# Products with C over two neighbouring PSUM banks, six of twelve on GpSimd, and an earlier turn of the last image, in a selective-scan and convolution hybrid

## The chip, the cores and the metric

The kernel runs on one core of a Trainium2 chip. The metric is the device time of one execution in microseconds (us); the kernel before was timed three times, and the median counts. The core's engines are named PE (TensorE), ACT (ScalarE), DVE (VectorE) and POOL (GpSimd); SP is the queue that issues every DMA here.

## The reference

Four images of 96 channels and 64 x 64 pixels go through four layers, and nothing is shared between images.

- Layer 0: group norm, a 1x1 projection to 192 channels and a depthwise 3x3 convolution with SiLU give u. u is read in four orders k: by rows (0), by columns (1), and both backwards (2 and 3). For each order and each of 192 channels a recurrence with 16 states runs over the 4096 positions. Then the four results, turned back to row order, are added, normalised and projected to 96 channels.

```python
delta = softplus(dts + dt_b)
dA    = exp(delta * A)                       # A is (order, channel, state)
h     = h * dA + (delta * u) * B[state]      # along the 4096 positions
y     = sum over states of h * C[state]  + Ds * u
```

- Layer 1: 1x1 expansion to 576 channels, depthwise 3x3 convolution, 1x1 projection, with a residual.
- Layer 2: layer norm, a 192-wide spectral block (Fourier transform over the positions, a diagonal complex product with ReLU, the inverse), then a feed-forward block 96-384-96 whose operands are rounded to 8-bit floats and whose sums are rounded to 16-bit floats.
- Layer 3: softmax-free attention, which is computed as a product with the sum of k v over all positions, and a second such feed-forward block.

## The kernel before

**The scan is cut into units and slots.** An order is scanned in 8 chunks of 512 positions, one chunk of one order of one image is a step, and a step has 12 units (`u` 0 to 11): there are 4 x 4 x 8 x 12 = 1536. A unit covers 128 rows (32 channel pairs times 4 states) and two channels `e` of a pair, so 2 x 512 elements in a row. `scans` (line 1120) writes the units out by hand, one a slot, in an order that no scheduler changes (line 1389). For slot `s` it issues in this order:

1. stores that were put off (`flush`, line 1266), then the loads of the next step's operands (`LOADS`, line 1164): each is a DMA of 512 KB that spreads `delta`, `du` or a pair of B and C rows over the 128 rows. The second B and C tile of a step is loaded at `u` 10, just ahead of its use.
2. `decays` of unit `s+1` on ACT (line 1180): for each `e` the last column of unit `s-1` is kept as the next chunk's start (`keep`, line 1203), then an exponential is written into a PSUM bank of its own out of four (`da`).
3. `product` of unit `s-1` on POOL (line 1215) if its `u` is in `POOL_C` = 1, 3, 6, 8, 10, and `inputs` of unit `s+2`, also on POOL (line 1176): `db` = delta u B, 128 x 1024.
4. `states` of unit `s` on DVE (line 1190): a scan for each `e`. For the other seven units of a step the scan is followed by the product with C, 128 x 512, for each `e` (line 1201).
5. `sums` on PE (line 1226) for a pair of units whose products were issued before; after the last pair of a pass ACT copies the result out (`yt`, line 1245), and its store is put off to the next slot's `flush`.

**Work beside the scan.** Everything else is written as generators grouped in stages (`plan`, line 1111): front of an image (its inputs to the scan), turn, conv, spectral, layer 2, layer 3. At the end of each slot `advance` (line 1353) takes steps from the stage at the head as long as their stated costs fit a budget for each engine (`SHARE`, line 55) and a total for the slot (`RATE`). Stages follow each other strictly; the stages of image b+1's front and of image b's later layers run beside scans of other images.

**The end.** Images are scanned in the orders 0, 1, 3, 2 (line 41). The turn (line 610) adds orders 0, 1 and 3 and the skip term of an image in row order, by matmuls with an identity, once three of its orders are scanned. `scan_outputs` (line 651) adds order 2 chunk by chunk, and the convolution takes two chunks at a time. For the last image the turn stands beside layer 3 of the third image, and its convolution is the last stage beside the scans; what is left of it, its spectral block, layer 2 and layer 3 run after the scan has ended, without a scan beside them (`alone`, line 1391). There all eight PSUM banks are handed out in turn, and in the feed-forward (line 856) ACT makes three passes for each of three 128-row parts: a copy to 16 bits (868), bias and ReLU (871), rounding to 8 bits (873).

Of the kernel before, what the change touches and what calls it, by code (L numbers as in the profile page):

```python
# [39 lines left out]

KORDER = (0, 1, 3, 2)

SCAN = {"rep_d": 3, "rep_g": 3, "rep_BC": 5, "db": 3, "hc": 5}
POOL_C = (1, 3, 6, 8, 10)
TMP, IN = 10, 5
# [8 lines left out]
RATE = 6.0  # L54
SHARE = {"pe": (3.0, 3.2), "act": (2.4, 3.0), "dve": (1.2, 1.7)}
NQ, NG, NPAIR = 4, HID // 32, H // 2
# [37 lines left out]
def hybrid_kernel(ctx: ExitStack, tc: tile.TileContext, a: dict):  # L94
# [15 lines left out]

    BANKS = {"mm": 3, "da": 4, "y": 1}

# [6 lines left out]
    def bank(tag="mm", turn=True):  # L119

        if alone and tag == "mm" and turn:
            tag = turns(alone)
        if tag == "mm":
            held_banks[0] += 1
        return psum.tile([128, CH], F32, name=f"ps_{tag}", tag=tag, bufs=BANKS[tag])

# [299 lines left out]

    def later(out, t):

        to_store.append((out, t))

    def flush():
        while to_store:
            store(*to_store.pop(0))

# [7 lines left out]

    def in_turn(items, make, matmuls, take, evict, depth=2):

        made = []

        def oldest():
            p, item, at = made.pop(0)
            yield take[:3] + (at,)
            evict(p, item)  # L450
            free()

        for n, item in enumerate(items):
            yield make[:3] + (n > 0,)
            p = bank()
            matmuls(p, item)
            made.append((p, item, clock[0]))
            if len(made) == depth:
                yield from oldest()
        while made:  # L460
            yield from oldest()
# [148 lines left out]
    def turn(b):  # L610

        im = b % 2
        while scanned[b] < 3 * NCH:
            yield wait(1)
        parts = [big("ya"), big("yb")]
        for lo in (0, 128):
            for t, k in zip(parts, (1, 3)):
                load(t[:, :L].rearrange("p (c l) -> p c l", c=NCH),
                     d_y[k][im][:, lo : lo + 128, :].rearrange("c p l -> p c l"))

            def fetch(c):
                y, u = (t[:, L + c % 4 * CH : L + c % 4 * CH + CH] for t in parts)
                load(y, d_y[0][im][c, lo : lo + 128])
                load(u[: min(128, DI - lo)], d_skip[b][c, lo : min(lo + 128, DI)])
                return y, u
# [5 lines left out]
            def added(p, of):  # L631
                c, (y, u) = of
                p = p[:m]
                for n, t in enumerate(parts):
                    rhs = t[:, :L].rearrange("p (w h) -> p h w", h=H)[:, c * RPC : (c + 1) * RPC, :]
                    mm(split(p), lhsT=add, rhs=rhs, start=n == 0, stop=False)
                mm(p, lhsT=add, rhs=y, start=False, stop=False)
                mm(p, lhsT=skip, rhs=u[: skip.shape[0]], start=False, stop=True)
# [5 lines left out]

            chunks = ahead(1, fetch, reversed(range(NCH)))
            first = next(chunks)
            yield wait(10)
            yield from in_turn(chain([first], chunks), pe(3.8, 1), added, ac(0.6), stored)
            yield wait(2)

    def scan_outputs(b, done):
# [3 lines left out]
        def fetch(c):  # L655
            out = []
            for of in (d_yt[b % 2][c], d_y[2][b % 2][c]):
                for part in (of[:128], of[128:]):
                    s = arrival("ypart")
                    load(s[: part.shape[0]], part)  # L660
                    out.append(s[: part.shape[0]])
            return out[0], out[2], out[1], out[3]

        coming = None
        for c in reversed(range(NCH)):
# [7 lines left out]
            for name, of in (("ident", parts[:2]), ("two", parts[2:])):  # L673
                yield pe(1.8, 1, name == "two")
                p = bank()
                for n, s in enumerate(of):
                    mm(p, lhsT=const(name, slice(0, s.shape[0])), rhs=s, start=n == 0, stop=n == 1)  # L677
                yield ac(0.6)
# [177 lines left out]
    def feed_forward(x, weights):  # L856
# [5 lines left out]
        for m in range(3):  # L862
# [6 lines left out]
            free()  # L869
            yield ac(0.65)  # L870
            act(acc, acc, AF.Relu, bias=bq[:, m : m + 1])  # L871
            yield ac(0.65)
            nc.scalar.activation(hq[:, m, :], acc, AF.Copy, saturate=False)  # L873
        yield pe(1.4, 1)
# [245 lines left out]
    def scans(stages):  # L1120
# [8 lines left out]
        for b in range(B):  # L1129
            for k in KORDER:  # L1130
                for n in range(NCH):
                    steps.append({"b": b, "k": k, "c": NCH - 1 - n if k >= 2 else n, "n": n, "BC": {}, "d": {}, "g": {}})
# [47 lines left out]
        def decays(x, last):  # L1180
            x["da"] = []
            for e in (0, 1):

                if last is not None:
                    keep(last, e)
                av = (x["step"]["k"] * NI + 2 * x["i"] + e) * NJ + x["j"]
                x["da"].append(bank("da"))
                act(x["da"][e], x["step"]["d"][x["i"]][:, e], AF.Exp, scale=aneg[:, av : av + 1])  # L1188

        def states(x):  # L1190
            step, u = x["step"], x["u"]
            order = slice(None, None, -1) if step["k"] >= 2 else slice(None)
            x["hc"] = pair("hc")
            x["h"] = [x["hc"][:, e] for e in (0, 1)] if x["pool"] else x["da"]
            for e in (0, 1):
                start = 0.0 if step["n"] == 0 else steps[x["number"] - 1]["last"][:, 2 * u + e : 2 * u + e + 1]
                nc.vector.tensor_tensor_scan(  # L1197
                    x["h"][e][:, order], x["da"][e][:, order], x["db"][:, e, order], start, ALU.mult, ALU.add
                )
                if not x["pool"]:  # L1200
                    x["made"] = nc.vector.tensor_mul(x["hc"][:, e], x["h"][e], x["step"]["BC"][x["j"]][:, 1])  # L1201

        def keep(x, e):
            step, u = x["step"], x["u"]
            if step["n"] < NCH - 1:
                if "last" not in step:
                    step["last"] = sp.tile([128, NI * NJ], F32, name="state")
                end = 0 if step["k"] >= 2 else CH - 1
                to = step["last"][:, 2 * u : 2 * u + 2]
                if not x["pool"]:  # L1210
                    nc.scalar.copy(to[:, e : e + 1], x["h"][e][:, end : end + 1])  # L1211
                elif e == 0:
                    nc.gpsimd.tensor_copy(to, x["hc"][:, :, end])  # L1213

# [11 lines left out]
        def sums(group):  # L1226
# [6 lines left out]
            for m in (1, 0):  # L1233
                x = group[m]
                for e in (1, 0):
# [3 lines left out]
                    if made is None:  # L1239
                        made = group[0]["made"]  # L1240
                        tc.add_manual_dep(done.ins, made.ins.name, mybir.DependencyInfo(
                            mybir.DependencyClass.Sync, mybir.DependencyReason.DATA), reason="sums")
            if last:
                yt = sp.tile([128, CH], F32, name="yt")
                nc.scalar.copy(yt, y)  # L1245
                to = d_y[step["k"]][step["b"] % 2][step["c"]]
                for m in (0, 1):
                    at = 128 * group[0]["pass"] + 64 * m
                    later(to[at : at + 64].rearrange("(p e) l -> e p l", e=2), yt[64 * m : 64 * m + 64])
                if group[0]["pass"] == 1:  # L1250
                    scanned[step["b"]] += 1

# [10 lines left out]
        for slot in range(len(units) + 6):  # L1263
            clock[0] = slot
            x = units[slot] if slot < len(units) else None
            flush()
            if x is not None:
# [10 lines left out]
                if x["number"] + 1 < len(steps) and x["u"] in LOADS:  # L1278
                    if x["u"] == 4:
                        need(steps[x["number"] + 1])  # L1280
                    fetch(steps[x["number"] + 1], LOADS[x["u"]])
            if slot + 1 < len(units):
                decays(units[slot + 1], units[slot - 1] if slot > 0 else None)
# [259 lines left out]
```

## Time and profile before

| what | value |
|---|---|
| time, median of 3 runs (lowest to highest) | 6703.26 us (6702.1 to 6710.55) |
| the profiled execution: its own time, its span | 6708.94 us, 6707.1 us |
| busy: PE, ACT | 4836.7 us (72%), 4357.4 us (65%) |
| busy: DVE, POOL | 5521.4 us (82%), 5173.5 us (77%) |
| DMA | 1121.42 MB, 167 GB/s over the span |
| first and last start of a DVE scan | 78.8 us, about 6126 us |

A time in the profile counts from the start of the span. A group of instructions is one line of the kernel on one engine with one kind of tiles: its busy time, the mean length of one, and the idle time of the engine just before them with what ended most of it. In a table by stretches each row is a stretch of the span with each engine's busy time in it and, in brackets, its instructions; then the clock granted to TensorE (1 is full), the share of the DMA engines' time in use and GB/s. POOL runs one `db` instruction (line 1178) for each unit, so the number of those in a stretch is its number of units.

### The profile page before, as it was taken

What the parts mean: (1) busy time and instruction counts of PE and PEld (TensorE: products, weight loads), DVE (VectorE), ACT (ScalarE), POOL (GpSimd) and SP (SyncE); (2) the same over time, 40 slices, a digit from 0 to 9 for tenths busy, and PEclk for the clock granted to TensorE, in tenths of its full rate; (3) what the DMA queues carried; (4) which work ended last, traced back from release to release, by engine and by line L of the source; (5) the groups of instructions that cost most, each with busy time, mean ns of one, the idle gap of its engine ahead of it and who ended that gap; (6) DMA issues with size and microseconds to landing.
All of it is one profiled execution on the core that took longest, in us unless ns stands there. A gap on an engine that the chain in (4) does not pass through costs nothing. (4 is left out here: it accounts for less than half of the span.)

```text
span 6707.1 us, 84452 instructions
## 1 busy us (share of the span) xinstructions
PE 4836.7 (72%) x27884; PEld 1777.4 (26%) x27884; DVE 5521.4 (82%) x5803; ACT 4357.4 (65%) x8296; POOL 5173.5 (77%) x2743
## 2 busy tenths in 40 slices
PE   7633857657987676775688777777887776779986
PEld 2100212111223531121122254221223532213562
DVE  5979899898999889889999988887999889895110
ACT  5743767765665577876556656866665677755367
POOL 4756878789999789977999988888999889894000
PEclk9755968768998787797799988878998887889997
DMA  5644555576644544455765454465644544563120
GB/s 185 193 157 142 180 188 188 180 239 231 188 152 143 181 154 145 156 187 187 257 208 165 147 168 167 144 208 176 193 151 151 193 157 145 202 230 101 38 82 27
DMA packets 438825, 1121.42 MB, mean 167 GB/s; under 512 B 73002, under 2 KB 74768, under 8 KB 437140
## 3 DMA queue, kind: packets, MB, share of 16 engines
q1 hardware_dynamic: 438388, 1116.02, 50.9%
q8 instruction: 222, 3.64, 0.2%
q14 instruction: 215, 1.76, 0.1%
HBM read 881.28 MB, written 239.01 MB: 167 GB/s over the span
## 5 line engine op out<-in xcount | busy, mean ns | idle before, releaser
L1178 POOL TENSOR_TENSOR db<-rep_g,rep_BC 128x1024 f32<-128x1024 f32 x1536 | 3600.2, 2364 | 551.0 <-DMA rep_BC<-bc 281.9
L1188 ACT ACTIVATE ps_da<-rep_d,aneg 128x512 f32<-128x512 f32 x3072 | 2067.3, 690 | 542.0 <-DVE hc L1197 404.5
L1197 DVE TENSOR_TENSOR_SCAN ps_da<-ps_da,state,db 128x512 f32<-128x512 f32 x1568 | 2007.1, 1280 | 237.3 <-ACT state L1211 154.5
L1216 POOL TENSOR_TENSOR hc<-hc,rep_BC 128x1024 f32<-128x1024 f32 x640 | 1510.8, 2361 | 91.0 <-DVE hc L1197 41.4
L1237 PE MATMUL ps_y<-hc,cst 128*32 128x512 f32 x6144 | 1026.7, 746 | 619.3 <-POOL hc L1216 348.2
L1197 DVE TENSOR_TENSOR_SCAN hc<-ps_da,state,db 128x512 f32<-128x512 f32 x1120 | 1371.1, 1266 | 70.3 <-ACT ps_da L1188 23.1
L1201 DVE TENSOR_TENSOR hc<-ps_da,rep_BC 128x512 f32<-128x512 f32 x1792 | 1239.2, 692 | 112.5 <-PE ps_y L1237 3.9
L1211 ACT COPY state<-ps_da 128x1 f32<-128x1 f32 x1568 | 247.2, 158 | 471.1 <-DVE hc L1201 466.3
L1237 PEld LDWEIGHTS ps_y<-hc,cst 128*32 128x32 f32 x6144 | 145.8, 119 | 1264.8 <-POOL hc L1216 556.6
L786 PE MATMUL ps_mm<-h,wd 128*32 128x512 f32 x3048 | 348.5, 593 | 7.0 <-ACT r L153 7.0
L1213 POOL COPY state<-hc 128x2 f32<-128x2 f32 x560 | 106.0, 189 | 306.9 <-DVE hc L1197 294.2
L531 PE MATMUL ps_mm<-xp,taps 128*128 128x512 f32 x576 | 293.6, 652 | 41.5 <-ACT xp L511 14.4
L1197 DVE TENSOR_TENSOR_SCAN ps_da<-ps_da,db 128x512 f32<-128x512 f32 x224 | 273.6, 1221 | 41.7 <-ACT state L1211 23.8
L582 PE MATMUL ps_mm<-xd,dtw 128*128 128x512 f32 x256 | 177.1, 783 | 162.2 <-ACT z L604 116.2
L763 PE MATMUL ps_mm<-wd,w 128*32 128x512 f32 x2032 | 261.2, 621 | 36.8 <-DMA wd<-x 11.9
L1245 ACT COPY yt<-ps_y 128x512 f32<-128x512 f32 x256 | 149.1, 582 | 151.1 <-PE ps_y L1237 145.1
L591 ACT ACTIVATE z<-ps_mm 128x512 f32<-128x512 f32 x192 | 114.3, 595 | 167.8 <-PE ps_mm L582 106.6
L912 PE MATMUL ps_mm<-wa,xp 128*64 128x96 f32 x1728 | 143.2, 327 | 103.1 <-DVE d L916 79.1
L597 DVE SCALAR_TENSOR_TENSOR ps_mm<-ps_mm,z 128x512 f32<-128x512 f32 x192 | 132.3, 689 | 99.1 <-ACT z L595 69.6
L1197 DVE TENSOR_TENSOR_SCAN hc<-ps_da,db 128x512 f32<-128x512 f32 x160 | 186.2, 1204 | 9.4 <-ACT ps_da L1188 9.0
L845 PE MATMUL ps_mm<-r,cst 128*128 128x512 f32 x206 | 138.8, 761 | 70.8 <-ACT acc L868 26.6
L569 PE MATMUL ps_mm<-ua,sel 128*128 128x512 f32 x128 | 101.3, 880 | 114.7 <-ACT z L604 91.1
(420 smaller groups left out, 6954.1 us busy)
## 6 DMA issues: line engine op xcount, KB each, us to landing
rep_BC<-bc SPq DMA_DIRECT2D x512, 512.0 KB
rep_g<-du SPq DMA_DIRECT2D x384, 512.0 KB
rep_d<-delta SPq DMA_DIRECT2D x384, 512.0 KB
y<-yt SPq DMA_DIRECT2D x512, 128.0 KB
du<-g SPq DMA_DIRECT2D x128, 256.0 KB
delta<-z SPq DMA_DIRECT2D x128, 256.0 KB
tab<-in_etab SPq DMA_DIRECT2D x128, 256.0 KB
du<-g SPq DMA_DIRECT2D x128, 128.0 KB
```

The source lines that it names most:

```text
L531: mm(p, lhsT=taps[:, t, 0:128], rhs=window(t, c + e), start=t == 0, stop=t == 8)
L582: mm(p, lhsT=dtw[:, o + 2 * part, 0:128], rhs=xd, start=True, stop=True)
L763: mm(p[32 * n : 32 * n + 32], lhsT=w1[:, 32 * g : 32 * g + 32], rhs=xin[:, n : n + 15 : 2, 1 : W + 1], start=True, stop=True)
L786: mm(p[32 * n : 32 * n + 32], lhsT=held["wd"][:, groups[i], o, dx, :], rhs=here[i][:, :, dx : dx + W], start=dx == 0, stop=dx == 2)
L1178: nc.gpsimd.tensor_mul(x["db"], x["step"]["g"][x["i"]], both(x["step"]["BC"][x["j"]][:, 0]))
L1188: act(x["da"][e], x["step"]["d"][x["i"]][:, e], AF.Exp, scale=aneg[:, av : av + 1])
L1197: nc.vector.tensor_tensor_scan(x["h"][e][:, order], x["da"][e][:, order], x["db"][:, e, order], start, ALU.mult, ALU.add)
L1201: x["made"] = nc.vector.tensor_mul(x["hc"][:, e], x["h"][e], x["step"]["BC"][x["j"]][:, 1])
L1211: nc.scalar.copy(to[:, e : e + 1], x["h"][e][:, end : end + 1])
L1216: x["made"] = nc.gpsimd.tensor_mul(x["hc"], x["hc"], both(x["step"]["BC"][x["j"]][:, 1]))
L1237: done = mm(y[32 * q : 32 * q + 32], lhsT=const("stack"), rhs=x["hc"][:, e], start=first or (x["pass"] == 0 and x["j"] == 0), stop=last or ...
L1245: nc.scalar.copy(yt, y)
```

## The change

- **Pairs of banks.** `da` becomes two buffers of two neighbouring banks each, one for a unit. Both exponentials of unit `s+1` now stand behind the whole of unit `s-1`; the last columns of both `e` are kept by one copy, and the product with C of a unit on DVE is one instruction of 128 x 1024 behind both scans. When no scan is beside, a `da` buffer gives one bank of its two, so that six banks are in turn.
- **Six products on POOL:** `u` 1, 3, 5, 7, 9, 11.
- **Loads ahead of stores:** `flush` moves behind the loads within a slot.
- **Budgets:** ACT's ceiling in a slot falls from 3.0 to 2.8, DVE's share rises from 1.2 to 1.5 and its ceiling from 1.7 to 2.0.
- **Last image:** its orders are scanned 1, 3, 0, 2. Its turn starts when orders 1 and 3 are done, and takes order 0 chunk by chunk as it comes; for channels 128 to 191 order 0 is added later, in `scan_outputs`, with one more load and matmul a chunk. A chunk counts as scanned when its store has been issued.
- **Feed-forward at the end:** with no scan beside, bias and ReLU go to DVE for all three parts, and the rounding to 8 bits for one of them.

```diff
-KORDER = (0, 1, 3, 2)
+KORDER = [(0, 1, 3, 2)] * (B - 1) + [(1, 3, 0, 2)]
-POOL_C = (1, 3, 6, 8, 10)
+POOL_C = (1, 3, 5, 7, 9, 11)
-SHARE = {"pe": (3.0, 3.2), "act": (2.4, 3.0), "dve": (1.2, 1.7)}
+SHARE = {"pe": (3.0, 3.2), "act": (2.4, 2.8), "dve": (1.5, 2.0)}
-    BANKS = {"mm": 3, "da": 4, "y": 1}
+    BANKS = {"mm": 3, "da": 2, "y": 1}
...
+        if tag == "da":
+            t = psum.tile([128, 2, CH], F32, name="ps_da", tag=tag, bufs=BANKS[tag])
+            return t[:, 0] if alone else t
...
     def turn(b):
-        while scanned[b] < 3 * NCH:
+        early = b == B - 1
+        while scanned[b] < (2 if early else 3) * NCH:
             yield wait(1)
...
-        for lo in (0, 128):
+        for lo in (128, 0) if early else (0, 128):
...
+            rows = not (early and lo == 128)
...
-                load(y, d_y[0][im][c, lo : lo + 128])
+                if rows:
+                    load(y, d_y[0][im][c, lo : lo + 128])
...
+            ready = (lambda n: scanned[b] >= 2 * NCH + min(n + 2, NCH)) if early and rows else (lambda n: True)
...
     def scan_outputs(b, done):
-            for of in (d_yt[b % 2][c], d_y[2][b % 2][c]):
-                for part in (of[:128], of[128:]):
...
+            yt, y0, y2 = (of[b % 2][c] for of in (d_yt, d_y[0], d_y[2]))
+            for part in (yt[:128], y2[:128], yt[128:], y2[128:]) + ((y0[128:],) if b == B - 1 else ()):
...
     def feed_forward(x, weights):
...
+            if alone:
+                yield dv(0.75)
+                nc.vector.tensor_scalar(acc, acc, bq[:, m : m + 1], 0.0, ALU.add, ALU.max)
+            else:
+                yield ac(0.65)
+                act(acc, acc, AF.Relu, bias=bq[:, m : m + 1])
+            if alone and m == 1:
+                yield dv(0.75)
+                nc.vector.tensor_copy(hq[:, m, :], acc, saturate=False)
+            else:
+                yield ac(0.65)
+                nc.scalar.activation(hq[:, m, :], acc, AF.Copy, saturate=False)
...
         def decays(x, last):
-            x["da"] = []
-            for e in (0, 1):
-                if last is not None:
-                    keep(last, e)
-                av = (x["step"]["k"] * NI + 2 * x["i"] + e) * NJ + x["j"]
-                x["da"].append(bank("da"))
-                act(x["da"][e], x["step"]["d"][x["i"]][:, e], AF.Exp, scale=aneg[:, av : av + 1])
+            if last is not None:
+                keep(last)
+            x["da"] = bank("da")
+            for e in (0, 1):
+                av = (x["step"]["k"] * NI + 2 * x["i"] + e) * NJ + x["j"]
+                act(x["da"][:, e], x["step"]["d"][x["i"]][:, e], AF.Exp, scale=aneg[:, av : av + 1])
...
         def states(x):
-                if not x["pool"]:
-                    x["made"] = nc.vector.tensor_mul(x["hc"][:, e], x["h"][e], x["step"]["BC"][x["j"]][:, 1])
+            if not x["pool"]:
+                x["made"] = nc.vector.tensor_mul(x["hc"], x["h"], both(x["step"]["BC"][x["j"]][:, 1]))
...
+                copy = nc.gpsimd.tensor_copy if x["pool"] else nc.scalar.copy
+                copy(step["last"][:, 2 * u : 2 * u + 2], x["h"][:, :, end])
...
             x = units[slot] if slot < len(units) else None
-            flush()
             if x is not None:
...
                     fetch(steps[x["number"] + 1], LOADS[x["u"]])
+            flush()
             if slot + 1 < len(units):
```

## The prediction

> **What bounds the kernel now.** I read the page's totals, then its groups, then a table by stretches, then two queues in order of time.
>
> ```profile
> PE 4836.7 (72%) x27884; PEld 1777.4 (26%) x27884; DVE 5521.4 (82%) x5803; ACT 4357.4 (65%) x8296; POOL 5173.5 (77%) x2743
> ```
>
> DVE leads and POOL is close behind, but the average spans stages of different kinds. What a unit costs on each engine is in the groups:
>
> ```profile
> L1178 POOL TENSOR_TENSOR db<-rep_g,rep_BC 128x1024 f32<-128x1024 f32 x1536 | 3600.2, 2364 | 551.0 <-DMA rep_BC<-bc 281.9
> ...
> L1197 DVE TENSOR_TENSOR_SCAN ps_da<-ps_da,state,db 128x512 f32<-128x512 f32 x1568 | 2007.1, 1280 | 237.3 <-ACT state L1211 154.5
> L1216 POOL TENSOR_TENSOR hc<-hc,rep_BC 128x1024 f32<-128x1024 f32 x640 | 1510.8, 2361 | 91.0 <-DVE hc L1197 41.4
> ...
> L1201 DVE TENSOR_TENSOR hc<-ps_da,rep_BC 128x512 f32<-128x512 f32 x1792 | 1239.2, 692 | 112.5 <-PE ps_y L1237 3.9
> L1211 ACT COPY state<-ps_da 128x1 f32<-128x1 f32 x1568 | 247.2, 158 | 471.1 <-DVE hc L1201 466.3
> ```
>
> POOL per unit: its busy time without 7 us of clearing, 5166/1536 = 3.36 us. DVE per unit is read from start to start, in order of time (start, length):
>
> ```profile
> 3641.93 1.29 DVE L1197 TENSOR_TENSOR_SCAN ps_da<-ps_da,state,db 128x512 f32<-128x512 f32 x1 [0.17 <-POOL db L1178]
> 3643.31 0.69 DVE L1201 TENSOR_TENSOR hc<-ps_da,rep_BC 128x512 f32<-128x512 f32 x1
> 3643.92 1.28 DVE L1197 TENSOR_TENSOR_SCAN ps_da<-ps_da,state,db 128x512 f32<-128x512 f32 x1
> 3645.23 0.69 DVE L1201 TENSOR_TENSOR hc<-ps_da,rep_BC 128x512 f32<-128x512 f32 x1
> 3645.84 2.45 DVE L1197 TENSOR_TENSOR_SCAN hc<-ps_da,state,db 128x512 f32<-128x512 f32 x2
> ```
>
> A unit with its product takes 3645.84 - 3641.93 = 3.91 us. One without takes 2.37 (the next such, from 3657.04, has its successor at 3659.41). So (7 x 3.91 + 5 x 2.37)/12 = 3.27 us, before work beside it. The table by stretches (length, busy PE, PEld, DVE, ACT, POOL, clock, DMA share, GB/s) shows which engine is full where:
>
> ```profile
> 663.00:1452.00 789.00, 533.32 (x1657) 147.44 (x1655) 712.13 (x761) 572.95 (x1074) 607.22 (x320) 0.81 0.58 187
> 1452.00:2090.00 638.00, 512.14 (x2595) 136.00 (x2598) 598.35 (x615) 384.68 (x768) 602.89 (x321) 0.89 0.59 195
> 2090.00:2291.00 201.00, 139.76 (x1734) 102.49 (x1730) 179.53 (x187) 110.97 (x212) 163.66 (x89) 0.79 0.48 159
> 2291.00:2834.00 543.00, 372.84 (x2147) 147.17 (x2140) 479.73 (x494) 421.03 (x805) 481.34 (x254) 0.78 0.48 156
> 4135.00:4585.00 450.00, 314.77 (x1036) 95.09 (x1033) 362.86 (x376) 311.06 (x611) 364.49 (x194) 0.80 0.52 172
> 6126.00:6319.00 193.00, 184.74 (x1248) 68.93 (x1240) 12.51 (x24) 70.06 (x109) 0.00 (x0) 0.98 0.11 32
> ```
>
> The rows are a front, turn and conv, spectral, layers 2 and 3, layer 3 with a turn, and the conv that is left when the scan has ended. In front DVE is at 90% and POOL at 77%; in turn and conv both are at 94%; elsewhere neither is over 90%; at the end PE is at 96%. With all such stretches and their units (the count of L1178 in each):
>
> | stage | us | units | us a unit |
> |---|---|---|---|
> | front | 1485 | 336 | 4.42 |
> | weights | 264 | 48 | 5.50 |
> | turn and conv, last scan | 2130 | 600 | 3.55 |
> | spectral | 679 | 168 | 4.04 |
> | layers 2 and 3 | 1039 | 276 | 3.76 |
> | layer 3 with turn | 450 | 108 | 4.17 |
>
> After 6126 us come conv 193, spectral 152, layer 2 139, layer 3 97 us.
>
> One more wait matters. First SP, then POOL, in order of time:
>
> ```profile
> 3616.67 3.07 SPq L1153 DMA_DIRECT2D rep_d<-delta  x2
> 3629.70 1.11 SPq L433 DMA_DIRECT2D y<-yt  x2
> 3630.92 0.56 SPq L1147 DMA_DIRECT2D rep_BC<-bc  x1
> ```
> ```profile
> 3635.68 2.38 POOL L1178 TENSOR_TENSOR db<-rep_g,rep_BC 128x1024 f32<-128x1024 f32 x1
> 3639.50 4.73 POOL L1178 TENSOR_TENSOR db<-rep_g,rep_BC 128x1024 f32<-128x1024 f32 x2 [1.44 <-DVE hc L1201]
> ```
>
> From 3619.7 SP stood in front of the `y` store until ACT had copied `yt` (3629.09 to 3629.68); the B/C load stood behind it, and POOL idled for the `db` that reads it. Counted by position in a step, 316 us of POOL's 551 us before `db` stand before that one, unit 2's.
>
> **What the Trainium skill says.** "VectorE: DVE Perf Modes", section on the TRN2 errata: an fp32 tensor_tensor takes (N+151)/0.96 ns. For 512 that is 691, the trace has 692; for 1024 it gives 1224 ns, my price of the merged product. "GPSIMD Engine Reference", 3.1: about 2.6 cycles an element for two inputs, so an estimate of 2.2 us for 1024 before dispatch; the trace has 2361 ns, which I use. "SBUF — State Buffer", Who interferes with whom: a DVE instruction with one SBUF input outside the two-port modes does not contend with GpSimd. The merged product reads C alone from SBUF, as now; the trace agrees in that `db` has minimum 2333 and median 2360 ns beside a busy DVE. I charge no contention.
>
> **The change part by part.**
>
> *POOL:* one product more in 12 units, 2361/12 = 197 ns, and 7/8 of a 189 ns state copy, 14 ns: 3.36 + 0.21 = 3.57 us a unit. With about 1% of waits, nothing goes below 3.60.
>
> *DVE:* a unit with a product now has its second scan 1.2 us behind the first, as in a unit without (2.45 us for two), the product 1.37 behind that (1.29 and the gap of 0.09 that the lines above show), and the next unit some 1.15 later (1.224 less the overlap of 0.08 that they show): 3.72 instead of 3.91. Six of each: (6 x 3.72 + 6 x 2.37)/12 = 3.05, so 0.22 us less. ACT's copies fall from 1568 to 672, 896 x 158 ns = 142 us or 0.09 a unit; its work is not what is full, so nothing.
>
> *By stage.* Turn and conv go onto POOL's floor: 3.55 to 3.60, +30 us. In layers 2 and 3 DVE waits for ACT and ACT for PE; of 0.22 the floor leaves 0.16, and I take 0.10, since these waits are uneven: -28. Layer 3 with turn is full of strided matmuls: -0.12, -13. Front is DVE's: I take 0.16 of 0.22, as PE to ACT chains hold part of it: -54. Spectral 0.14: -24. Weights 0.15: -7. Sum -96. DVE's larger share moves work within the front, without a change of the sum: nothing.
>
> *Loads ahead of stores:* today DVE waits only some 59 us for `db`, so the 316 us cost little; once POOL is the bound they would be paid in full. With the load ahead of the store, and its buffer freed by DVE at `u` 8 rather than POOL, I take them as gone, which is in the floor's 1%. If that cover fails, up to 316 us come back. The other way round, stores leave at most a few instructions later; their readers are a scan later: nothing.
>
> *The pair as a wait:* ACT's exponentials for unit s+1 stand behind DVE's whole unit s-1, 1.3 to 1.9 us later than the first of them today; behind them queue ACT's beside work, and DVE waits for them. DVE's next unit lasts at least 2.4 us and the first exponential needs 0.16 + 0.69, so ACT may be late by 1.5 us before it shows. Today DVE waits about 269 us before scans for ACT, some 170 times by the table of waits; each could grow by 1.3, or none. Bounds 0 and +220; no gain, since nothing starts earlier. POOL's floor hides most outside the front: +30.
>
> *The turn of the last image:* the same 16 chunks, one 128 KB load and one matmul moved per chunk. It leaves the last scan's start and joins layer 3 of the third image in some 50 units, where the last turn of that kind cost 0.4 a unit more (4.17 against 3.76): +20.
>
> *The end.* In the built program, PE has 84 matmuls of the depthwise kind fewer after the last scan (240 against 324), 68 of the expansion (148 against 216), one output stage and two norms. By the chain of waits (two records for each fp32 matmul), 12 of the first take 2.58 us, 12 of the second 2.61, an output stage 7.0: 18 + 15 + 7 + 2 = -42, one to one as PE is 96% full there. In layers 2 and 3, 48 ReLU (735 ns) and 16 roundings (633 ns) leave ACT, 45 us, of which with three chunks at a time some 37 are on the path; on DVE, 93% idle there, a 16-bit tensor_scalar of 512 costs an estimated 290 ns (four elements a cycle and 150 cycles, same page, perf-mode tier table; no run shows it). The chain gains two handovers a part: I take -25. Six banks for eight: a bank comes round after four, not eight; bounds 0 and about 25 us if norms stall; +10. Sum -57.
>
> Total -96 + 30 + 20 - 57 = -103 us. The sum is made against the profiled execution, 6708.94 us, and gives 6606; the runs' median is 5.7 us lower, so 6600.
>
> **The rivals.** (1) *The pair's wait decides, slower.* ACT reaches 3.2 us a unit in layers 2 and 3, so it is often late by more than 1.5 us. The 170 waits grow by 1.3 each and little of it is hidden: 6600 - 30 + 200 = 6770. For it: L1211's 471 us idle for DVE. Against: most of that is ACT being early. Chance 0.13. (2) *Everything freed is used:* no coupling, no cost of the moved turn, POOL's DMA waits gone, and all 0.22 outside POOL's floor: each stage at the larger of 3.60 and its old time less 0.22 gives +30 - 44 - 24 - 74 - 37 - 11 = -160 in the scan, -57 at the end: 6486. For it: 316 us at one place. Chance 0.2. (3) *No net in the scan:* DVE was not what front and spectral wait for, so relief there only pays POOL's extra and the coupling; the end alone gains, and bank stalls take half: 6703 - 30 = 6675 to 6703, say 6690. For it: ACT waits for PE in front. Chance 0.14. That the change doesn't do what it says is no rival: the built program has 768 products of 128 x 1024 on POOL and 768 on DVE.
>
> **How the numbers follow.** My forecast has 0.53. Its own range is 6550 to 6660. The range for 8 in 10 reaches up over rival 3 and down to most of rival 2: 6490 to 6710. About 0.2% (13 us) is what a measurement can tell. Faster by more: forecast, rival 2 and a third of rival 3, 0.77; within: 0.10; slower: 0.13.
>
> **What would show it.** Right: in conv stretches POOL is at 98% or more and a unit takes 3.58 to 3.63; `db` of unit 2 no longer waits; front units near 4.25; the merged product at about 1224 ns; under 155 us of conv after the last scan; ACT under 135 us in the last two layers. Wrong: DVE's wait for ACT's exponentials above 400 us in all, POOL's products over 2.4 us, or B/C waits that stay.

## The result and the profile after

The kernel after takes 6788.23 us (median of 4 runs, 6776.42 to 6794.54) against 6705.88 us for the kernel before (median of 4, taken beside it): a ratio of 1.012, 95% interval 1.0107 to 1.0133. The prediction said 6600, with a range up to 6710. The change costs 82 us. One run of `a_single` (11137.62 us) and one of `b_pairs` (7224.32 us) below fell in a slow state and are left out of their ratios, and their traces are not read.

The totals of the page of after, to be read against the same line of before:

```profile
PE 4867.1 (72%) x27884; PEld 1763.9 (26%) x27884; DVE 5342.9 (79%) x4843; ACT 4326.1 (64%) x7336; POOL 5485.2 (81%) x2983
```

DVE has 179 us less work, as intended, and POOL 312 us more. The time grew all the same, so DVE waits more. The groups of after (busy us, mean ns | idle us before them, and what ended most of it) show where:

```profile
L1210 POOL TENSOR_TENSOR db<-rep_g,rep_BC 128x1024 f32<-128x1024 f32 x1536 | 3597.4, 2361 | 162.5 <-DVE ps_da L1228 82.2
...
L1228 DVE TENSOR_TENSOR_SCAN ps_da<-ps_da,state,db 128x512 f32<-128x512 f32 x1344 | 1729.9, 1287 | 482.8 <-ACT ps_da L1219 295.8
L1244 POOL TENSOR_TENSOR hc<-hc,rep_BC 128x1024 f32<-128x1024 f32 x768 | 1811.6, 2359 | 144.8 <-DVE hc L1228 63.0
...
L1232 DVE TENSOR_TENSOR hc<-ps_da,rep_BC 128x1024 f32<-128x1024 f32 x768 | 940.6, 1225 | 63.2 <-DMA weights<-in_rows 0.4
...
L1241 ACT COPY state<-ps_da 128x2 f32<-128x2 f32 x672 | 106.1, 158 | 510.5 <-DVE hc L1232 509.9
```

`db` waits 162.5 us where it waited 551.0, and POOL's instructions are as long as before (2361 and 2359 ns for 2364 and 2361), so no slowing of one engine by the other shows. The merged product takes 1225 ns. But the largest scan group waits 482.8 us for 237.3, although it has fewer scans. The table of waits names the engine (who waited for whom: us in total, times, longest). Before, then after:

```profile
DVE ps_da L1197 <- ACT state L1211: 178.4, 98, 7.0
...
DVE ps_da L1197 <- ACT ps_da L1188: 36.1, 32, 4.4
...
DVE hc L1197 <- ACT ps_da L1188: 32.0, 21, 5.7
...
DVE hc L1197 <- ACT state L1211: 22.9, 16, 7.5
```
```profile
DVE ps_da L1228 <- ACT ps_da L1219: 331.8, 179, 9.0
...
DVE hc L1228 <- ACT ps_da L1219: 182.1, 96, 9.3
```

Before, that is 269 us for the exponentials and the state copies among them; after, 514 us for the exponentials alone. The stretches of after answer to the rows of before (length, busy PE, PEld, DVE, ACT, POOL, clock, DMA share, GB/s):

```profile
650.00:1456.00 806.00, 533.00 (x1615) 146.45 (x1617) 660.63 (x616) 561.09 (x943) 605.57 (x328) 0.80 0.55 179
1456.00:2112.00 656.00, 513.16 (x2580) 134.75 (x2579) 564.42 (x485) 377.43 (x659) 627.91 (x347) 0.88 0.56 184
2112.00:2292.00 180.00, 132.02 (x1728) 96.59 (x1724) 163.57 (x150) 106.16 (x166) 164.60 (x87) 0.84 0.52 174
2292.00:2844.00 552.00, 371.33 (x2145) 145.69 (x2146) 467.83 (x403) 428.82 (x736) 519.61 (x287) 0.79 0.48 156
4160.00:4636.00 476.00, 345.58 (x1158) 104.64 (x1159) 378.32 (x330) 337.83 (x590) 424.81 (x234) 0.79 0.52 177
6278.00:6430.00 152.00, 141.08 (x934) 51.53 (x927) 9.23 (x17) 51.19 (x79) 2.37 (x1) 0.97 0.12 34
```

With their units (169, 177, 45, 146, 118) these are 4.77, 3.71, 4.00, 3.78 and 4.03 us a unit; before, 4.38, 3.54, 4.19, 3.77, 4.17. In the front DVE has fallen from 90% to 82% busy, and a unit takes 0.39 us more. In turn and conv POOL is at 96% (627.91 of 656). The scan ends at 6278 us for 6126, a loss of 152; what follows it takes 511 us for 581, a gain of 70.

### The profile page after: what moved, and what is told of

Read it like the earlier page. It is cut to its first block, busy times and chain, and to the rows that moved or that the text cites. A ratio compares the mean times of both kernels' runs of the same rounds, so it can differ in the third digit from the quotient of the medians.

```text
span 6789.7 us, 82982 instructions
## 1 busy us (share of the span) xinstructions
PE 4867.1 (72%) x27884; PEld 1763.9 (26%) x27884; DVE 5342.9 (79%) x4843; ACT 4326.1 (64%) x7336; POOL 5485.2 (81%) x2983
## 5 line engine op out<-in xcount | busy, mean ns | idle before, releaser
L1210 POOL TENSOR_TENSOR db<-rep_g,rep_BC 128x1024 f32<-128x1024 f32 x1536 | 3597.4, 2361 | 162.5 <-DVE ps_da L1228 82.2
L1219 ACT ACTIVATE ps_da<-rep_d,aneg 128x512 f32<-128x512 f32 x3072 | 2119.5, 691 | 495.1 <-DVE hc L1228 317.3
L1228 DVE TENSOR_TENSOR_SCAN ps_da<-ps_da,state,db 128x512 f32<-128x512 f32 x1344 | 1729.9, 1287 | 482.8 <-ACT ps_da L1219 295.8
L1244 POOL TENSOR_TENSOR hc<-hc,rep_BC 128x1024 f32<-128x1024 f32 x768 | 1811.6, 2359 | 144.8 <-DVE hc L1228 63.0
L1228 DVE TENSOR_TENSOR_SCAN hc<-ps_da,state,db 128x512 f32<-128x512 f32 x1344 | 1645.9, 1266 | 197.7 <-ACT ps_da L1219 163.3
L1232 DVE TENSOR_TENSOR hc<-ps_da,rep_BC 128x1024 f32<-128x1024 f32 x768 | 940.6, 1225 | 63.2 <-DMA weights<-in_rows 0.4
L1241 POOL COPY state<-hc 128x2 f32<-128x2 f32 x672 | 126.9, 189 | 488.0 <-DVE hc L1228 451.2
L1241 ACT COPY state<-ps_da 128x2 f32<-128x2 f32 x672 | 106.1, 158 | 510.5 <-DVE hc L1232 509.9
L1228 DVE TENSOR_TENSOR_SCAN ps_da<-ps_da,db 128x512 f32<-128x512 f32 x192 | 235.5, 1226 | 71.9 <-ACT ps_da L1219 36.0
L1228 DVE TENSOR_TENSOR_SCAN hc<-ps_da,db 128x512 f32<-128x512 f32 x192 | 223.5, 1205 | 24.0 <-ACT ps_da L1219 18.8
L790 ACT ACTIVATE h<-ps_mm 128x512 f32<-128x512 f32 x266 | 151.7, 593 | 35.0 <-PE ps_mm L786 33.2
```

Of the source, the lines that this page charges most:

```text
L790: act(h[:, :, 1 : W + 1], split(p), AF.Relu)
L1210: nc.gpsimd.tensor_mul(x["db"], x["step"]["g"][x["i"]], both(x["step"]["BC"][x["j"]][:, 0]))
L1219: act(x["da"][:, e], x["step"]["d"][x["i"]][:, e], AF.Exp, scale=aneg[:, av : av + 1])
L1228: nc.vector.tensor_tensor_scan(x["h"][:, e, order], x["da"][:, e, order], x["db"][:, e, order], start, ALU.mult, ALU.add)
L1232: x["made"] = nc.vector.tensor_mul(x["hc"], x["h"], both(x["step"]["BC"][x["j"]][:, 1]))
L1241: copy(step["last"][:, 2 * u : 2 * u + 2], x["h"][:, :, end])
```

## The experiments

Theory P was the prediction's first rival, the pair as a wait; Q, that six products on POOL are the cost; F, the new place of loads and stores; S, the budgets. "Alone" below means against the kernel named. All times are medians of three to twelve runs; each comparison with the kernel before is good to some 0.15%, 10 us.

**Undoing one part of the kernel after at a time.** Four single banks again, `a_single`:

```diff
-            if not x["pool"]:
-                x["made"] = nc.vector.tensor_mul(x["hc"], x["h"], both(x["step"]["BC"][x["j"]][:, 1]))
+                if not x["pool"]:
+                    x["made"] = nc.vector.tensor_mul(x["hc"][:, e], x["h"][e], x["step"]["BC"][x["j"]][:, 1])
...
-            if last is not None:
-                keep(last)
-            x["da"] = bank("da")
             for e in (0, 1):
+                if last is not None:
+                    keep(last, e)
...
+                x["da"].append(bank("da"))
```

> The kernel after with four single banks for da again: each exponential, scan, product on DVE (128x512) and last column on ACT by itself; six products still on POOL. Theory P (the pair as a wait: ACT's exponentials behind the whole of unit s-1 make DVE wait, 514 us in all against some 269 before): at least 100 us come back, 6690 or less, and DVE's waits for ACT fall towards 270 us. Theory Q (six products on POOL: POOL is the bound and PE's sums stand behind its product, 739 us against 348): the pair was a gain by itself, so the time stays within 30 us of 6788 or grows. Theory F (loads ahead of stores) and theory S (budgets): no change beyond 30 us.

6701.98 us, ratio 0.9996 (0.9987 to 1.0005): the pair costs 86 us, as much as the whole loss, though less than the 100 that theory P asked for.

```diff
-POOL_C = (1, 3, 5, 7, 9, 11)
+POOL_C = (1, 3, 6, 8, 10)
```

> The kernel after with five products on POOL (u 1, 3, 6, 8, 10). Theory Q: POOL falls from 3.57 to 3.37 us a unit, and 60 to 150 us come back: 6640 to 6730; PE's wait for POOL's product falls from 739 towards 350 us. Theory P: DVE has 1.35/12 = 0.11 us a unit more work and is as late as before, so 6788 to 6900. F, S: within 30 us of 6788.

6830.6 us, 1.0189 (1.0173 to 1.0206). Q fell: with the pair, six products on POOL are 42 us better than five. The edit changes which units they are as well as how many, and `a_even` below shows that the choice of units alone can be worth 53 us, so number and place aren't told apart here.

```diff
             x = units[slot] if slot < len(units) else None
+            flush()
...
-            flush()
             if slot + 1 < len(units):
```

> The kernel after with stores ahead of loads in a slot again. Theory F (stores behind loads delay the loads and stores of the work beside, for which PE and ACT then wait): 50 us or more come back, 6740 or less, although POOL's wait for the B and C tile returns. Theories P, Q, S: POOL's 316 us of waits before one db return and now count, as POOL is near its bound: 6800 to 7000.

6821.49 us, 1.0183 (1.0168 to 1.0199). F fell: loads ahead of stores are a gain, 33 us here.

```diff
-SHARE = {"pe": (3.0, 3.2), "act": (2.4, 2.8), "dve": (1.5, 2.0)}
+SHARE = {"pe": (3.0, 3.2), "act": (2.4, 3.0), "dve": (1.2, 1.7)}
```

> The kernel after with the budgets of before (ACT's ceiling 3.0, DVE's share 1.2 and ceiling 1.7). Theory S (more of DVE's beside work in one slot makes uneven slots, which POOL and ACT can't make up): 50 us or more come back, 6740 or less. Theories P, Q, F: within 30 us of 6788.

6744.48 us, 1.0067 (1.005 to 1.0084): the budgets cost 44 us, which the prediction had at nothing.

**What in the pair costs.** First both undone together, then the wait that the prediction named put onto single banks, the other six units on POOL, and the pair alone on the kernel before.

`a_single_share` has the edits of `a_single` and `a_share`:

> The kernel after with four single banks again and the budgets of before; six products on POOL, loads ahead of stores, the earlier turn and the end stay. If the two costs (86 us for the pair, 44 us for the budgets, each undone alone) are separate, 6788 - 86 - 44 = 6658. If both are one thing (DVE late for ACT's exponentials, once because they start late, once because DVE's beside work comes between), 6690 to 6702. Theory Q (six on POOL as such is a cost): not under 6690.

6671.59 us, 0.9954 (0.994 to 0.9969). The two costs are mostly separate; 30 of the 44 us of the budgets remain without the pair. `a_share` and this kernel differ by the pair alone, and the starts of units in their traces show where it costs: 21 us in the fronts (336 units), 21 in layers 2 and 3 (251 units), and no more than 6 in turn and conv (602 units), where POOL is nearly full.

```diff
+                done = act(x["da"][e], ...
+                if e == 0 and last is not None:
+                    tc.add_manual_dep(done.ins, last["end"].ins.name, ...
```

Here `last["end"]` is DVE's last instruction of unit s-1.

> Four single banks, one scan, product and last column for each e as in the kernel before, and six products on POOL (6702 without more), with one wait added: the first exponential of unit s+1 waits for DVE's last instruction of unit s-1, as the pair makes it. Theory P (the wait is what the pair costs): 6788 or more, since DVE doesn't have the merged product's gain: 6780 to 6900. If the merged instructions themselves cost (the second scan starts 1.2 us behind the first, the product comes in one piece): 6700 to 6720.

6711.25 us, 1.0012 (1.0002 to 1.0022). Theory P as the prediction put it fell: to start the exponentials behind the whole of unit s-1 costs 9 us, hardly more than the comparison can tell.

```diff
-POOL_C = (1, 3, 5, 7, 9, 11)
+POOL_C = (0, 2, 4, 6, 8, 10)
```

> The kernel after with u 0, 2, 4, 6, 8, 10 on POOL for 1, 3, 5, 7, 9, 11. A pair of units is summed two slots after its second unit; with even units POOL's product of a pair is issued one slot earlier. Theory Q2 (PE stands in its sums for POOL's product, 739 us, and what stands behind it on PE and ACT is late): 40 us or more come back, 6750 or less, and PE's wait for POOL's product falls below 300 us. Theory P: 6788 within 30 us.

6841.57 us, 1.0206 (1.0189 to 1.0223). PE's wait for POOL's product fell from 739 to 208 us, and the time grew by 53. Taking that wait away brought no time back. Why even units are worse is open.

`b_pairs` makes the edit of `a_single` the other way round, in the kernel before:

> The kernel before with pairs of banks alone (merged product and last columns; exponentials behind the whole unit s-1); five products on POOL, the order, the budgets, the turn and the end as before. The working of the prediction: DVE 0.19 x 7/12 = 0.11 us a unit less, some -90 us and +30 for the wait: 6640. Theory P: the pair costs as much as it did in the kernel after, +40 to +120 us: 6745 to 6825.

6813.92 us (the median of its three other runs), 1.0165 (1.0145 to 1.0185): 110 us, where the prediction's working gave some -60.

The late starts of scans gave the next theory. In order of time, ACT and then DVE of the kernel after:

```profile
5720.31 0.68 ACT L1092 ACTIVATE xc<-ps_mm,cols 96x512 f32<-96x512 f32 x1 [8.74 <-PE ps_mm L1090]
5720.90 1.40 ACT L1219 ACTIVATE ps_da<-rep_d,aneg 128x512 f32<-128x512 f32 x2
```
```profile
5722.39 2.46 DVE L1228 TENSOR_TENSOR_SCAN hc<-ps_da,state,db 128x512 f32<-128x512 f32 x2 [7.19 <-ACT ps_da L1219]
```

and of the kernel before:

```profile
744.36 0.70 ACT L1188 ACTIVATE ps_da<-rep_d,aneg 128x512 f32<-128x512 f32 x1
744.99 0.16 ACT L1211 COPY state<-ps_da 128x1 f32<-128x1 f32 x1
745.02 1.92 ACT L1188 ACTIVATE ps_da<-rep_d,aneg 128x512 f32<-128x512 f32 x3
```
```profile
745.16 1.29 DVE L1197 TENSOR_TENSOR_SCAN ps_da<-ps_da,state,db 128x512 f32<-128x512 f32 x1 [1.82 <-ACT state L1211]
```

Before, the scan starts 0.1 us after the first exponential has ended (745.06), while the second still runs. (The profile names the copy, which ended later, at 745.15; but late scans without a copy there also start 0.08 to 0.1 us after the first exponential.) After, the two exponentials end at 5722.30, and only then, at 5722.39, does the first scan start, though it reads the first alone. Counted over the trace, 467 of 1536 first scans of before start ahead of the end of their second exponential, and none of after; 390 of after start within 0.2 us of that end, having waited over 0.15 us each and 648 us in all. The built program says why: the two halves are one tile, and its waits are set for the tile as a whole, so a pair's first scan waits for both exponentials and the second for nothing more from ACT. For the same reason the second exponential waits until the first has ended, and the second of two scans into one `da` tile until the first has. This is theory T. Single banks were given these waits one by one.

```diff
+                x["end"] = nc.vector.tensor_tensor_scan(
...
+                if e == 0:
+                    tc.add_manual_dep(x["end"].ins, x["exp"].ins.name, ...
```

Here `x["exp"]` is the unit's second exponential.

> Four single banks and six products on POOL (6702 without more), with one wait added: a unit's first scan also waits for its second exponential, as it does in the kernel after, where no scan starts before it has ended (467 of 1536 units do in the kernel before). Theory T (the two halves of a pair are one tile to whoever sets the waits, so the first scan starts an exponential, 0.69 us, later whenever ACT is late): about 400 late starts by 0.7 us are 280 us at most, part of it hidden: 6750 to 6810. If this wait costs nothing: 6702 to 6712.

6736.0 us, 1.0045 (1.0029 to 1.0062): 34 us, less than I expected, but clear. By the same count 400 first scans now start late at the end of the second exponential (44 in `a_single_wait` and 46 in `a_single_share`, which lack the wait).

`a_single_both_wait` adds the edit of `a_single_wait`:

> The same with both waits of the pair: the first scan behind the second exponential, and the first exponential behind DVE's last instruction of unit s-1. Theory T: the waits are all that the pair costs, and here DVE lacks the merged product's gain, so 6788 or more, up to 6850. If the merged instructions themselves cost: 6705 to 6740.

6744.69 us, 1.0061 (1.0045 to 1.0077). The two waits are 43 of 86 us; neither expectation was met.

```diff
+                if e == 0:
+                    x["exp0"] = x["exp"]
+                else:
+                    tc.add_manual_dep(x["exp"].ins, x["exp0"].ins.name, ...
```

> Four single banks and six products on POOL with the two waits of the pair (6745) and a third: the second exponential waits until the first has ended, as the pair makes it (1416 ns for both against 1307 without it). Theory T: each of some 390 late first scans starts another 0.11 us later, up to 43 us: 6765 to 6790. If this is not what is left of the pair's cost: 6745 within 10 us.

6775.35 us, 1.0104 (1.0089 to 1.0119): 31 us more. The three waits make 73 of the 86 us, without one instruction being merged. (The steps of 34, 9 and 31 were added in this order; each has an uncertainty of about 10.) The six banks at the end are some 5 to 13 more: what follows the scan takes 504 to 511 us in the traces of `a_first` and `after`, and 498 to 500 in those of `a_single_wait`, `a_single_both_wait` and `a_single_all`, which have the same budgets and eight banks. What is left is within the uncertainty: the merged product's gain, less its second scan's wait for the first, doesn't show. That last wait, and the one copy for both last columns, were not put on single banks by themselves.

**The other parts.** `a_single_share_five` has the edits of `a_single`, `a_share` and `a_five`; `b_flush` makes the edit of `a_flush` the other way round in the kernel before.

> Four single banks, budgets of before, five products on POOL: that is the kernel before with loads ahead of stores, the earlier turn and the new end alone. The end is worth some 66 us (515 us after the last scan against 581). If the sixth product on POOL is a gain without the pair too (42 us with it): 6690 to 6720 against 6672. If it is a cost there (POOL at its bound in turn and conv, PE behind it): 6630 to 6665.

> The kernel before with loads ahead of stores alone. If POOL's 316 us before unit 2's db were hidden there, as the prediction took them: 6690 to 6710, with these waits gone. If they were paid in part, as in the kernel after (33 us): 6650 to 6685. If late stores cost the work beside: over 6715.

6657.91 us, 0.993 (0.9916 to 0.9945), and 6656.31 us, 0.9928 (0.9913 to 0.9943). Two things follow. Loads ahead of stores alone gain 47 us against 6703. And turn, order and end together gain nothing, though what follows the scan is 62 us shorter: 61 us are lost in the scan, by the starts of units in the two traces 23 at the turn of image 0, 24 at that of image 1 and 26 at that of the last, less some 13 that come back between them. The first two turns were not meant to change. PE in order of time at the first turn, `a_single_share_five`, and SP's issue of the load that PE waits for:

```profile
1485.15 1.89 PE L653 MATMUL ps_mm<-yb,cst 128*128 128x512 f32 x2
1498.10 2.07 PE L655 MATMUL ps_mm<-ya,cst 128*128 128x512 f32 x2 [11.05 <-DMA ya<-y]
```
```profile
1488.19 0.58 SPq L640 DMA_DIRECT2D ya<-y  x1
```

PE stands 11.05 us in front of a 128 x 512 tile that was asked for only when the turn's first matmuls were out. `a_first` (on the kernel after) and `a_best` (on `a_single_share_five`) put the early request back:

```diff
+            first = [] if early and rows else [next(chunks)]
             yield wait(10)
-            yield from in_turn(chunks, pe(3.8, 1), ...
+            yield from in_turn(chain(first, chunks), pe(3.8, 1), ...
```

> The kernel after with one thing put back: in a turn, the load of the first chunk's row-order tile and skip operand is issued before the wait of ten slots, as in the kernel before, and not when the first matmuls are issued (for order 0 of the last image, which isn't there yet, it stays). Theory R (PE stands in its queue for these loads; the scan lost 23 us at the turn of the first image and 24 at that of the second against a kernel without the new turn, 10 to 14 us at each of two places): 6788 - 45 = 6743, from 6735 to 6755. If the slower turns come from the order of the chunks (0 to 7 for 7 to 0): 6788 within 10 us.

> Four single banks, five products on POOL, budgets of before, the first load of a turn issued early again: of the change only loads ahead of stores, the earlier turn of the last image and the new end. Theory R: 6658 - 45 = 6613 (6605 to 6625). Otherwise 6650 to 6665.

6756.82 us, 1.0074 (1.0057 to 1.0091), and 6622.15 us, 0.9873 (0.9859 to 0.9888): 31 and 36 us come back, the first 2 us short of what was expected. The change also turned the order of a turn's chunks round (0 to 7 for 7 to 0) for every image, which its description doesn't name; both kernels keep that, so it isn't the cause. PE at the same place of `a_best`:

```profile
1483.66 1.90 PE L653 MATMUL ps_mm<-yb,cst 128*128 128x512 f32 x2
1485.37 1.17 PE L655 MATMUL ps_mm<-ya,cst 128*128 128x512 f32 x2
```

The two follow each other without a wait. `a_best` beats both kernels.

```diff
-SHARE = {"pe": (3.0, 3.2), "act": (2.4, 2.8), "dve": (1.5, 2.0)}
+SHARE = {"pe": (3.0, 3.2), "act": (2.4, 3.0), "dve": (1.5, 2.0)}
```

> The kernel after with ACT's ceiling in a slot back at 3.0; DVE's budget stays at 1.5 and 2.0. If ACT's lower ceiling is what the budgets cost (44 us together): 6735 to 6755. If DVE's larger share is: 6775 to 6795.

6797.85 us, 1.0135 (1.012 to 1.0151), a little above the range for DVE's share. ACT's ceiling is not the cost, DVE's share is. The traces suggest how. From the first to the last matmul of line 598 for the second image's front takes 335 us in the kernel after and 336 in `a_share`, but 67 units are scanned in it for 72; the next two fronts have the same sign (69 and 70 units for 75 and 73). The front takes its time; the larger share only lets it run beside fewer units. Units from the last image's turn to the end of the scan are 138 for 116: what was moved ahead leaves slots at the end that have to be scanned all the same. What follows the scan is 12 us shorter for it (511 for 523), the scan 60 longer.

```diff
+            if alone:
+                yield dv(0.75)
+                nc.vector.tensor_scalar(acc, acc, bq[:, m : m + 1], 0.0, ALU.add, ALU.max)
...
```

This is the end's feed-forward put into `b_flush`:

> The kernel before with loads ahead of stores and the feed-forward's passes on DVE at the end; five products, single banks, the old order of the last image and the old turns. By the stretches of the last layers (217 us with the new end against 251) it gives 6656 - 34 = 6622. If the earlier turn is a gain of its own (29 us less conv after the last scan, some 18 us more beside the scan), this is about 11 us slower than the 6622 of the version with it: 6625 to 6640; if not, 6610 to 6622.

6625.81 us, 0.9883 (0.9867 to 0.99): the feed-forward on DVE is worth 31 us, and the earlier turn with the new order of the last image, 6622 (`a_best`) against 6626, no more than the measurement can tell.

`a_best_six` is `a_best` with the six units of the change:

> The version of 6622 us with six products on POOL (u 1, 3, 5, 7, 9, 11) for five. If the sixth product is a small cost where the banks are single, as 6672 against 6658 said: 6630 to 6645. If that difference was chance, or a gain once nothing else holds the scan: 6590 to 6625.

6640.11 us, 0.9901 (0.9886 to 0.9916): 18 us slower; `a_single_share` against `a_single_share_five` said 14. Without the pair the sixth product is a cost. The totals of `a_single_share_five`, then of `a_single_share`:

```profile
PE 4852.3 (73%) x27884; PEld 1778.4 (27%) x27884; DVE 5541.5 (83%) x5867; ACT 4314.1 (65%) x8232; POOL 5180.2 (78%) x2743
```
```profile
PE 4845.0 (73%) x27884; PEld 1757.5 (26%) x27884; DVE 5383.8 (81%) x5611; ACT 4271.5 (64%) x8008; POOL 5488.2 (82%) x2983
```

DVE is relieved of 158 us, POOL gets 308, and the time rises. The sum hides two opposite effects. By the starts of the same units in the traces (the stages bounded as in the kernel before), five products against six:

| traces | fronts, 336 units | turn and conv of images 0 and 1, 362 units |
|---|---|---|
| `a_best`, `a_best_six` | 1481, 1460 us | 1268, 1305 us |
| `a_single_share_five`, `a_single_share` | 1482, 1464 us | 1315, 1335 us |

In the fronts, where DVE is the fuller engine, six products are a gain of 0.05 to 0.06 us a unit. In turn and conv, where POOL is nearly full, they cost more than that: 3.50 becomes 3.60 us a unit in the first pair of traces. I read this as DVE's relief and POOL's load; the products' places in a step change with their number, and were not tried apart.

## Why the prediction was wrong, point by point

From the kernel before to the kernel after there is a chain of measured kernels, each one part further: 6703 - 47 (loads ahead, `b_flush`) - 31 (feed-forward, `b_flush_ff`) - 4 (turn and order, `a_best`) + 36 (late first load, `a_single_share_five`) + 14 (sixth product, `a_single_share`) + 30 (budgets, `a_single`) + 86 (pair, `after`) = 6787. As differences along a chain they must add up; what they show is the share of each part in this order. Other orders share it out somewhat differently (33 for 47, 31 for 36, 44 for 30, -42 for +14).

- **The pair** is the step that failed most. I took the first exponential behind the whole of unit s-1 as its one new wait, +30, and the merged product as a gain that more than pays for it. That wait measured 9. I did not ask what else waits for a tile of two halves: the first scan for the second exponential (34), the second exponential for the end of the first (31). Rival 1 had the right object, the right sign and nearly the time (6770), and its mark, over 400 us of DVE waiting for ACT, came true with 514; but its wait was the smallest of the three, so that its time came near was luck.
- **The merged unit's length.** I took 3.72 us, with the second scan 1.2 behind the first. In order of time, DVE of the kernel after:

```profile
3654.81 2.62 DVE L1228 TENSOR_TENSOR_SCAN ps_da<-ps_da,state,db 128x512 f32<-128x512 f32 x2 [0.51 <-POOL db L1210]
3657.52 1.23 DVE L1232 TENSOR_TENSOR hc<-ps_da,rep_BC 128x1024 f32<-128x1024 f32 x1
3658.66 2.45 DVE L1228 TENSOR_TENSOR_SCAN hc<-ps_da,state,db 128x512 f32<-128x512 f32 x2
```

  From 3654.81 to 3658.66 are 3.85 us. The two scans into one `da` tile take 2.62, those of a POOL unit 2.45, mostly because the second waits for the end of the first. The product itself came as priced by the Trainium skill ("VectorE: DVE Perf Modes", section on the TRN2 errata): its formula gives an estimate of 1224 ns, and 1225 were measured. The gain is 0.06 us a unit with a product (medians 3.902 before and 3.847 after), not 0.19.
- **DVE's 0.22 us a unit as time, -96 us.** Six merged units of twelve were to give 0.09 of the 0.22 and gave 0.03. The other 0.13 is the product that moves to POOL, and its worth in the fronts is 0.05 to 0.06 us a unit, as the table above shows. So "Front is DVE's" was right in part: I counted about three quarters of DVE's relief there as time, and less than half came. In the kernel after even that doesn't show, as the pair and the budgets stand against it: the second image's front takes 329 us before and 335 after. Rival 3 ("DVE was not what front and spectral wait for") was right at most in part, and it didn't see that the change would cost something besides.
- **POOL's floor**, 3.57 worked out and 3.60 taken, was right: 3.60 us a unit in turn and conv of `a_best_six`. In the kernel after they take 3.71 at 96%, part of which is the late first load. What was off is what it was compared with: today's 3.55 still held the waits that go with the loads ahead of the stores, and without them five products take 3.50 (`b_flush`). So the sixth product costs 0.10 there, not 0.05.
- **DVE's larger share "moves work within the front, without a change of the sum: nothing"**: it cost 30 to 44 us.
- **Loads ahead of stores**: I let POOL's 316 us count for nothing until POOL is the bound, and for all of it then. Alone, the new place was worth 47 us, and in the kernel after 33. The waits went as said: in the table of waits of after, POOL's wait for the B and C tile is 11 us (281.9 before).

```profile
POOL db L1210 <- DMA rep_BC<-bc: 11.0, 3, 5.4
```

- **The turn.** "The same 16 chunks, one 128 KB load and one matmul moved per chunk" missed a line of the diff that touches all turns: the first request no longer goes out ahead of the stage's wait. 36 us. The cost of the moved turn itself, +20, was about right (the scan ends 18 us later in `a_best` than in `b_flush_ff`, of which 26 come at the last turn, while 8 are gained before it).
- **The end was right.** Conv after the scan took 152 us, as 193 - 42 gives (161 in `a_best`, where the budgets of before leave more of it to the end); the feed-forward gained 31 where I took 25; six banks cost 5 to 13 where I took 10. The 16-bit tensor_scalar took 349 ns, against 290 estimated from the Trainium skill ("VectorE: DVE Perf Modes", perf-mode tier table).
- **A reading.** "Elsewhere neither is over 90%" is not so for one stretch that isn't shown: in the last spectral stage beside the scans (5092 to 5372 us) DVE is busy for 260.12 of 280 us, 93%. No term of the sum hangs on it.

Not tried: a merged product over two banks whose halves have waits of their own. So whether the merged product would gain by itself is open; so is why even units are worse, why six products are better than five beside the pair and worse without it, and what sets the front's 335 us, which I take to be its own chains between PE, ACT and DVE, but didn't measure apart.

## What to carry to other kernels

Before two buffers are made one, list every instruction that reads or writes half of it, and give each the waits of both halves; that list, not the saved instruction, is the price. Relief of an engine at 90% came back by less than half here, and was lost again in the stages where the engine that took the work over was nearly full: compare the same units, stage by stage, in two traces that differ by this alone, and not the totals. And read a diff for lines that are shared by cases which the change doesn't mean, such as the moment of a first load.

## What the runs showed of the hardware

Two instructions of one engine, of which the second waits for the first's completion, cost some 0.1 us more than two that don't. Medians in the trace of `after`: the second scan of a pair into `da` starts 35 ns behind the end of the first, the second scan of a POOL unit, which has no such wait, 82 ns ahead of it. Two exponentials with nothing between them on ACT take 1416 ns from start to end in `after` and 1299 in `a_single_both_wait`, which lacks the wait. A 128 x 512 load asked for by PE's next matmul was 9.9 us away (issued at 1488.19, its matmul at 1498.10, in `a_single_share_five`).
